# A thresholding layer between convolutions: the mixing unit takes one matrix for two images instead of two matrices for one image

## The chip, the cores and the metric

The kernel runs on one core of one Trainium2 chip, in one launch. The core has a matrix engine (TensorE, PE in the profile, with its weight loads listed apart as PEld), a vector engine (VectorE, DVE), a scalar engine (ScalarE, ACT), a general engine (GpSimd, POOL), and a queue that issues the DMA transfers (SyncE, SP). Each takes its instructions in order, and they wait for one another by semaphores. TensorE writes its products to PSUM, which has eight banks of 512 fp32 values in each of 128 partitions; everything else lies in SBUF or in DRAM. The metric is the device time of one execution in microseconds (us).

## What is computed

Four images of 64 channels of 256 x 256 values, all fp32, pass through four layers. Layers 0, 2 and 3 are long convolutions: every channel is convolved with a filter that is an outer product of a row filter and a column filter, so the kernel multiplies with two triangular Toeplitz matrices, and adds `x * bias`. Layer 1 is the one that the change touches. It goes to Haar coefficients, mixes the channels there with two 64 x 64 matrices, thresholds, and comes back:

```python
f1 = haar2d(x)
acc = jnp.zeros_like(f1[:, :conv_w.shape[1]])
for i in range(v.shape[0]):                      # two matrices
    f3 = f1 * v[i]
    f4 = jnp.einsum('bchw,oc->bohw', f3, conv_w[i])
    f5 = jnp.sign(f4) * jax.nn.relu(jnp.abs(f4) - tau[i])
    acc = acc + f5
y = haar2d(acc, inverse=True)
return y + x
```

Since `v[i]` and `tau[i]` depend on the place in the image alone and not on the channel, the kernel mixes first and multiplies with `v` afterwards; and the `+ x` is added as coefficients, before the inverse transform.

## The kernel before

Phase A is layer 0 and the forward Haar transform. It works in rounds of two channels of a pair of images (64 rounds, 32 for each pair, which is called a group). In a round the matrix engine multiplies with the row and the column filters (`toeplitz`, L307), ScalarE copies the first product to SBUF (L450), VectorE adds the residual (L470), GpSimd does the transform along the free dimension (`forward_free`, L355 and L357, sixteen operations from 128x1024 down to 128x8), TensorE does the other direction (`haar`, L319), and the result is copied out of PSUM (L483, by VectorE for a part of the rounds) and stored to a DRAM tensor `coef` (L488). Every store goes in four transfers of 64 partitions with 4 KB in a piece.

Phase B is the mixing. It needs all channels of one place, so it reads `coef` back in steps: a step is 128 partitions (two rows of the image times 64 channels) by two images by 512 values, 512 KB, 64 steps for each group. A step loads `f` (tile ft, four buffers, L546), `v` and `tau` (three buffers each, L552), and is cut into two units. In a unit of the kernel before, four matrix products (`mix`, L592) apply both matrices to one image; each occupies a 64 x 64 quarter of the array, and TensorE runs each as two instructions. Then follow `multiply` with v on VectorE, in place in PSUM (L603), the sign on ScalarE to an SBUF tile m (L609), the magnitude on ScalarE, in place in PSUM (L612), `less` on VectorE (subtraction of tau, in place in PSUM, L616), and `threshold` on VectorE, which multiplies the clipped magnitude with the sign into m (L619). The PSUM tile f4 has two buffers of two banks. It is called f in the profile, since digits are left out of names there. Of the two matrices' results one lies in the wrong half of the partitions, so for each step ScalarE copies the two halves of the second results crosswise into a tile `other` (`exchange`, L625, two copies of 64x1024), and GpSimd adds the first results and `f` (L629) and then `other` (L632) into a tile gt, which is stored to a DRAM tensor `mixed` (L635).

Phase C is the inverse transform with layers 2 and 3, again in rounds of two channels: it loads `mixed` (tile g, L699, four transfers of 256 KB), undoes the transform on GpSimd (`inverse_free`, L392) with scalings on ScalarE (L375) and on TensorE (L319, copies L728), runs four sets of Toeplitz products (c1r, c1c, c2r, c2c), with copies of ch on ScalarE (L740) and residuals on VectorE (L759), and stores the output (L766).

The order of the work is written out by hand. Every phase is a list of pieces, and `beside` issues the pieces of a main list with those of a side list spread evenly among them. As engines take their instructions in order, this order decides who stands behind whom. Phase A of the first group runs with the filter networks beside it; from round 34 on phase B of group 0 runs beside phase A of the second group; then phase C of group 0 starts, and phase B of group 1 runs beside it; the rest is phase C alone. A piece of phase B is named (u, j) here, with u the unit and j from 0 to 2, and s = u // 2 its step:

```python
(u, 0): mix(u), less(u - 1)
(u, 1): multiply(u), sign(u), threshold(u - 1); load(s + 2) in even units, add_second(s - 1) in odd ones
(u, 2): magnitude(u); exchange and add_first(s - 1) in even units, store(s - 1) in odd ones
```

The second half of the exchange stands at (u, 0) of odd units. A round of phase A is 10 pieces and one of phase C is 18. Copies out of PSUM and residuals of the phases A and C are put off to the start of the next piece (`later` and `flush`). Their PSUM tiles have four buffers of one bank (`acps`).

Of the kernel before, what the change touches and what calls it, by code (L numbers as in the profile page):

```python
# [41 lines left out]
F32 = mybir.dt.float32  # L42
# [5 lines left out]
P = 128  # L48
# [41 lines left out]
def conv_haar_kernel(  # L90
# [9 lines left out]
    def coefficients(name):  # L100
        return dram.tile([STEPS, 2, C, NB, 2, N], F32, tag=name, name=name)
# [166 lines left out]
    def copy_tau(k):  # L268
        tau_sb = thresholds[1]
        for i in range(2):  # L270

            at, half = taus.offset + (k * 2 + i) * W, 2 * W * COPIES
            by_row = [[half, 2]] if i == 0 else [[-half, 2]]
            to = bass.AP(taus.tensor, at + i * half, [[2 * half, C]] + by_row + [[1, W]])
            nc.sync.dma_start(to, tau_sb[:, 2 * i : 2 * i + 2].rearrange("p h k -> p (h k)"))
# [139 lines left out]
    def rows_of(dram_tile, c, bp):  # L415

        n = NB * W
        at = dram_tile.offset + (bp * 2 * C + c) * n
        return bass.AP(dram_tile.tensor, at, [[4 * C * n, ROW // 2], [C * n, 2], [1, n]])

    def all_rows(grp_tile, c0, images):

        parts = images.rearrange("p (s n) k -> p s (n k)", s=2)
        return [(rows_of(grp_tile, c0 + e, bp), parts[half(e), bp]) for e in range(CI) for bp in range(2)]
# [104 lines left out]
    def phase_b(grp):  # L529
# [7 lines left out]
        def step_of(ap, s):  # L537
            n = NB * W
            return bass.AP(ap.tensor, ap.offset + 2 * s * C * n, [[n, P], [1, n]])
# [14 lines left out]
        def four(name):  # L554

            tiles = [st[s][name] for s in range(2)]
            tiles.append(bp.tile([P, NB, W], F32, tag="other", name=f"spare_{name}_{grp}", bufs=2))
            return [t[:C, :, bass.ts(h, N)] for t in tiles for h in range(2)]

        def join():  # L560

            a, b, c, d, t, u = four("f")
# [9 lines left out]
        def part():  # L572

            a, b, c, d, t, u = four("g")
# [10 lines left out]
        def mix(u):  # L585
            f = st[u // 2]["f"]
            un[u]["f4"] = bps.tile([P, 2, W], F32, tag="f4", name=f"f4_{grp}_{u}")

            for i in range(2):
                for q in range(2):  # L590
                    to = (q + i) % 2
                    nc.tensor.matmul(  # L592
                        un[u]["f4"][half(to), i, :],
                        mixers[0][half(q), bass.ts(i, C)],
                        f[half(q), u % 2],
                        start=True,
                        stop=True,
                        tile_position=(q * ROW, to * ROW),
                    )

        def multiply(u):
            f4 = un[u]["f4"]
            nc.vector.tensor_tensor(f4, f4, st[u // 2]["v"], ALU.mult)  # L603
# [356 lines left out]
```

## Time and profile before

| what | us |
|---|---|
| three timed runs | 2892.87, 2900.72, 2903.77 |
| median of them | 2900.72 |
| profiled execution | 2902.61 |
| its span, first to last instruction | 2900.8 |
| PE busy, of the span | 2439.5 |
| POOL busy | 1930.3 |
| DVE busy | 1561.7 |
| ACT busy | 1523.6 |
| DMA queue q1, mean share of 16 engines | 76.3% |

Single instructions of phase B, from the groups of instructions with their shapes kept apart:

| instruction | count | mean ns |
|---|---|---|
| mix, PE, 64*64 64x512 | 2048 | 662 |
| multiply, DVE, 128x1024 | 256 | 1225 |
| sign, ACT, 128x1024 | 256 | 1029 |
| magnitude, ACT, 128x1024 | 256 | 1035 |
| less, DVE, 128x1024 | 256 | 1230 |
| threshold, DVE, 128x1024 | 256 | 1213 |
| copy of other, ACT, 64x1024 | 256 | 1046 |
| each of the two adds, POOL, 128x1024 | 128 | 2363 |

A line of a list of instructions in the profile gives the engine, the line of the kernel, the operation, what is written and what is read, and the count; in brackets stands how long the engine had been idle before and what it waited for. A line of a list of waits gives the waiting instruction, what it waited for, the total, how many times, and the longest. "issue" means that the engine waited for nothing that the profile shows. The granted clock is the share of full speed that TensorE was allowed, and the DMA share is the mean busy share of the core's 16 DMA engines.

### The profile page before, as it was taken

What the parts mean: (1) busy time and instruction counts of PE and PEld (TensorE: products, weight loads), DVE (VectorE), ACT (ScalarE), POOL (GpSimd) and SP (SyncE); (2) the same over time, 40 slices, a digit from 0 to 9 for tenths busy, and PEclk for the clock granted to TensorE, in tenths of its full rate; (3) what the DMA queues carried; (4) which work ended last, traced back from release to release, by engine and by line L of the source; (5) the groups of instructions that cost most, each with busy time, mean ns of one, the idle gap of its engine ahead of it and who ended that gap; (6) DMA issues with size and microseconds to landing.
All of it is one profiled execution on the core that took longest, in us unless ns stands there. A gap on an engine that the chain in (4) does not pass through costs nothing.

```text
span 2900.8 us, 119451 instructions
## 1 busy us (share of the span) xinstructions
PE 2439.5 (84%) x53276; PEld 1966.7 (68%) x53276; DVE 1561.7 (54%) x1765; ACT 1523.6 (53%) x2361; POOL 1930.3 (67%) x2294
## 2 busy tenths in 40 slices
PE   6999886777776777868978888888888999999999
PEld 5777775444444544546757767666677889898888
DVE  2453333777777777537656766666673333333333
ACT  1222222666776666436767776666674333433332
POOL 2787674977887877738767766766675556555551
PEclk9999998988998888979999999999999999999999
DMA  5878888899999999777989888888975555655552
GB/s 153 238 212 228 235 237 228 244 284 289 296 291 284 276 300 281 217 182 224 252 238 251 252 231 248 239 243 242 253 211 159 142 151 137 155 143 146 146 141 92
DMA packets 239673, 636.27 MB, mean 219 GB/s; under 512 B 39078, under 2 KB 121671, under 8 KB 223032
## 3 DMA queue, kind: packets, MB, share of 16 engines
q1 hardware_dynamic: 239160, 628.62, 76.3%
q8 instruction: 420, 6.88, 1.0%
q14 instruction: 93, 0.76, 0.1%
HBM read 413.12 MB, written 215.35 MB: 217 GB/s over the span
## 4 chain that ended last, share of the span: by engine, by line
PE 45%; ACT 11%; DMA 10%; issue 8%; DVE 7%; POOL 4%; SPq 2%; ACTq 0%; DVEq 0%; POOLq 0%
PE c1r L307 9%; PE c1c L307 9%; PE c2c L307 9%; PE c2r L307 8%; PE f L592 4%; PE c0ps L319 3%; DVE f L603 3%; ACT m L609 3%; ACT f L612 3%; DMA v<-in_v 3%; ACT other L625 2%; DMA ft<-coef 2%; POOL fw L355 1%; POOL f L357 1%; ACT ch L740 1%
## 5 line engine op out<-in xcount | busy, mean ns | idle before, releaser
L392 POOL TENSOR_TENSOR i<-i,g 128x16 f32<-128x16 f32 x744 | 393.1, 549 | 407.5 <-ACT g L375 397.7
L616 DVE TENSOR_TENSOR f<-f,tau 128x1024 f32<-128x1024 f32 x256 | 314.8, 1230 | 384.0 <-ACT f L612 384.0
L592 PE MATMUL f<-ft,mix 64*64 64x512 f32 x2048 | 341.1, 662 | 189.4 <-DVE m L619 102.0
L609 ACT ACTIVATE m<-f 128x1024 f32<-128x1024 f32 x256 | 263.3, 1029 | 415.8 <-DVE f L603 400.3
L307 PEld LDWEIGHTS a1ps<-tx,x 64*64 64x64 f32 x8192 | 332.7, 144 | 146.9 <-ACT f L483 65.6
L629 POOL TENSOR_TENSOR gt<-m,ft 128x1024 f32<-128x1024 f32 x128 | 302.5, 2363 | 192.9 <-DVE m L619 167.0
L307 PE MATMUL a1ps<-tx,x 64*64 64x256 f32 (+3 forms) x8192 | 363.5, 320 | 56.1 <-ACT f L483 26.0
L307 PE MATMUL c2r<-tx,cy 64*64 64x128 f32 (+3 forms) x8192 | 332.1, 305 | 50.2 <-issue 36.8
L307 PE MATMUL c1r<-tx,z 64*64 64x192 f32 (+3 forms) x8192 | 338.5, 308 | 39.2 <-issue 39.2
L307 PEld LDWEIGHTS c2r<-tx,cy 64*64 64x64 f32 x8192 | 308.9, 137 | 81.4 <-issue 48.7
L603 DVE TENSOR_TENSOR f<-f,v 128x1024 f32<-128x1024 f32 x256 | 313.6, 1225 | 91.8 <-PE f L592 64.8
L307 PEld LDWEIGHTS c1r<-tx,z 64*64 64x64 f32 x8192 | 316.3, 139 | 68.8 <-issue 51.1
L307 PEld LDWEIGHTS c1c<-ty,ch 64*64 64x64 f32 x8192 | 307.7, 135 | 64.8 <-ACT z L728 47.3
L632 POOL TENSOR_TENSOR gt<-gt,other 128x1024 f32<-128x1024 f32 x128 | 302.4, 2363 | 70.6 <-ACT other L625 68.1
L307 PE MATMUL c2c<-ty,ch 64*64 64x128 f32 (+3 forms) x8192 | 323.2, 298 | 27.5 <-issue 25.2
L307 PE MATMUL c1c<-ty,ch 64*64 64x256 f32 (+3 forms) x8192 | 335.3, 303 | 10.9 <-ACT z L728 8.8
L307 PEld LDWEIGHTS a2ps<-ty,ay 64*64 64x64 f32 x8192 | 301.5, 137 | 62.1 <-issue 35.4
L307 PEld LDWEIGHTS c2c<-ty,ch 64*64 64x64 f32 x8192 | 304.0, 134 | 50.5 <-issue 31.2
L307 PE MATMUL a2ps<-ty,ay 64*64 64x192 f32 (+3 forms) x8192 | 328.3, 304 | 10.2 <-issue 6.4
L740 ACT COPY ch<-c1r 128x512 f32<-128x512 f32 x256 | 137.6, 590 | 371.4 <-PE c1r L307 371.0
L470 DVE SCALAR_TENSOR_TENSOR x<-x,bias_sb,a2ps 128x512 f32<-128x512 f32 x256 | 179.4, 741 | 268.4 <-PE a2ps L307 252.3
L619 DVE SCALAR_TENSOR_TENSOR m<-f,m 128x1024 f32<-128x1024 f32 x256 | 310.5, 1213 | 0.1
(66 smaller groups left out, 3257.9 us busy)
## 6 DMA issues: line engine op xcount, KB each, us to landing
coef<-f SPq DMA_DIRECT2D x256, 256.0 KB, 4.9
ft<-coef SPq DMA_DIRECT2D x128, 512.0 KB, 9.1
v<-in_v SPq DMA_DIRECT2D x128, 512.0 KB, 10.0
tau<-taus SPq DMA_DIRECT2D x128, 512.0 KB, 10.6
mixed<-gt SPq DMA_DIRECT2D x128, 512.0 KB, 7.8
g<-mixed SPq DMA_DIRECT2D x256, 256.0 KB, 6.9
x<-in_x SPq DMA_DIRECT2D x63, 1024.0 KB, 9.7
out<-o SPq DMA_DIRECT2D x63, 1024.0 KB, 4.8
```

What stands on the lines that cost most here:

```text
L307: nc.tensor.matmul(ps[r][half(c), j % 2, k * ROW :], data[half(r), c, k, bass.ts(j, ROW)], t(r, c)[:, : N - k * ROW], start=k == 0, stop=k ...
L319: nc.tensor.matmul(ps[r][half(c)].rearrange("p h k -> p (h k)"), matrix[half(r)], pairs(r, c).rearrange("p h k -> p (h k)"), start=True, s ...
L392: engine.tensor_tensor(to, s, d, op)
L470: nc.vector.scalar_tensor_tensor(to, old, bias_sb[:, c : c + 1], ps, ALU.mult, ALU.add)
L592: nc.tensor.matmul(un[u]["f4"][half(to), i, :], mixers[0][half(q), bass.ts(i, C)], f[half(q), u % 2], start=True, stop=True, tile_position ...
L603: nc.vector.tensor_tensor(f4, f4, st[u // 2]["v"], ALU.mult)
L609: nc.scalar.activation(un[u]["m"], un[u]["f4"], AF.Sign)
L616: nc.vector.tensor_tensor(f4, f4, st[u // 2]["tau"], ALU.subtract)
L619: nc.vector.scalar_tensor_tensor(un[u]["m"], un[u]["f4"], 0.0, un[u]["m"], ALU.max, ALU.mult)
L629: nc.gpsimd.tensor_tensor(st[s]["g"], st[s]["m"][:, :, 0], st[s]["f"], ALU.add)
L632: nc.gpsimd.tensor_tensor(st[s]["g"], st[s]["g"], st[s]["other"], ALU.add)
L740: later(lambda y=y, ps=ps: nc.scalar.copy(y, ps))
```

## The change

A unit now applies one matrix, i = u % 2, to both images of a step. The product with v goes from PSUM to a new SBUF tile x (two buffers), with v broadcast over the images; sign and magnitude read x. The magnitude goes to a PSUM tile of its own, `a`, of two banks; f4 and `a` have one buffer each. The result tile m belongs to one unit (three buffers). What is exchanged between the halves is the second image's f, a copy of two times 64x512 in a step, and no longer the result. To make this fit, the matrix of the forward transform is permuted for one image, so that its two rows of a pair stand in exchanged halves, and v and tau are no longer laid out with reversed rows. Coefficients lie in DRAM as two steps side by side, so that a channel's piece in the store of `coef` and in the load of `mixed` is 8 KB in two transfers of a round; a step of phase B reads and writes 4-KB pieces at a distance of 8 KB. The pieces are issued in another order. The first steps' join of the low coefficients is made for each image, and starts with three steps loaded.

```diff
     def coefficients(name):
-        return dram.tile([STEPS, 2, C, NB, 2, N], F32, tag=name, name=name)
+        return dram.tile([STEPS // 2, 2, C, 2, NB, 2, N], F32, tag=name, name=name)
...
     def all_rows(grp_tile, c0, images):
-        parts = images.rearrange("p (s n) k -> p s (n k)", s=2)
-        return [(rows_of(grp_tile, c0 + e, bp), parts[half(e), bp]) for e in range(CI) for bp in range(2)]
+        n = 2 * NB * W
+        pairs = []
+        for e in range(CI):
+            at = grp_tile.offset + (c0 + e) * n
+            rows = bass.AP(grp_tile.tensor, at, [[2 * C * n, ROW // 2], [C * n, 2], [1, n]])
+            pairs.append((rows, images[half(e)].rearrange("p n k -> p (n k)")))
+        return pairs
...
         def step_of(ap, s):
             n = NB * W
-            return bass.AP(ap.tensor, ap.offset + 2 * s * C * n, [[n, P], [1, n]])
+            return bass.AP(ap.tensor, ap.offset + (s // 2 * P * 2 + s % 2) * n, [[2 * n, P], [1, n]])
...
         def mix(u):
-            f = st[u // 2]["f"]
-            un[u]["f4"] = bps.tile([P, 2, W], F32, tag="f4", name=f"f4_{grp}_{u}")
-            for i in range(2):
-                for q in range(2):
-                    to = (q + i) % 2
+            s, i = divmod(u, 2)
+            un[u]["f4"] = bps.tile([P, NB, W], F32, tag="f4", name=f"f4_{grp}_{u}", bufs=1)
+            for b in range(NB):
+                for r in range(2):
+                    q = r ^ b
                     nc.tensor.matmul(
-                        un[u]["f4"][half(to), i, :],
-                        mixers[0][half(q), bass.ts(i, C)],
-                        f[half(q), u % 2],
+                        un[u]["f4"][half(q), b, :],
+                        mixers[0][half(r), bass.ts(i, C)],
+                        st[s]["f"][half(r), b],
...
         def multiply(u):
-            f4 = un[u]["f4"]
-            nc.vector.tensor_tensor(f4, f4, st[u // 2]["v"], ALU.mult)
+            un[u]["x"] = bp.tile([P, NB, W], F32, tag="x", name=f"x_{grp}_{u}", bufs=2)
+            nc.vector.tensor_tensor(un[u]["x"], un[u]["f4"], both(u, "v"), ALU.mult)

         def sign(u):
-            if u % 2 == 0:
-                st[u // 2]["m"] = bp.tile([P, NB, 2, W], F32, tag="m", name=f"m_{grp}_{u}", bufs=2)
-            un[u]["m"] = st[u // 2]["m"][:, u % 2]
-            nc.scalar.activation(un[u]["m"], un[u]["f4"], AF.Sign)
+            un[u]["m"] = bp.tile([P, NB, W], F32, tag="m", name=f"m_{grp}_{u}", bufs=3)
+            nc.scalar.activation(un[u]["m"], un[u]["x"], AF.Sign)

         def magnitude(u):
-            nc.scalar.activation(un[u]["f4"], un[u]["f4"], AF.Abs)
+            un[u]["a"] = bps.tile([P, NB, W], F32, tag="a", name=f"a_{grp}_{u}", bufs=1)
+            nc.scalar.activation(un[u]["a"], un[u]["x"], AF.Abs)

         def less(u):
-            f4 = un[u]["f4"]
-            nc.vector.tensor_tensor(f4, f4, st[u // 2]["tau"], ALU.subtract)
+            nc.vector.tensor_tensor(un[u]["a"], un[u]["a"], both(u, "tau"), ALU.subtract)
...
-        def exchange(s, q):
-            if q == 0:
-                st[s]["other"] = bp.tile([P, NB, W], F32, tag="other", name=f"other_{grp}_{s}", bufs=2)
-            nc.scalar.copy(st[s]["other"][half(q)], st[s]["m"][half(1 - q), :, 1])
-
-        def add_first(s):
-            st[s]["g"] = bp.tile([P, NB, W], F32, tag="gt", name=f"gt_{grp}_{s}", bufs=3)
-            nc.gpsimd.tensor_tensor(st[s]["g"], st[s]["m"][:, :, 0], st[s]["f"], ALU.add)
-
-        def add_second(s):
-            nc.gpsimd.tensor_tensor(st[s]["g"], st[s]["g"], st[s]["other"], ALU.add)
+        def exchange(s):
+            st[s]["other"] = bp.tile([P, W], F32, tag="other", name=f"other_{grp}_{s}", bufs=2)
+            for q in range(2):
+                nc.scalar.copy(st[s]["other"][half(q)], st[s]["f"][half(1 - q), 1])
+
+        def add(u):
+            s, i = divmod(u, 2)
+            m = un[u]["m"]
+            if i:
+                nc.gpsimd.tensor_tensor(st[s]["g"], st[s]["g"], m, ALU.add)
+            else:
+                g = st[s]["g"] = bp.tile([P, NB, W], F32, tag="gt", name=f"gt_{grp}_{s}", bufs=3)
+                nc.gpsimd.tensor_tensor(g[:, 0], m[:, 0], st[s]["f"][:, 0], ALU.add)
+                nc.gpsimd.tensor_tensor(g[:, 1], m[:, 1], st[s]["other"], ALU.add)
+            un[u].clear()
...
+        def piece(u, j):
+            s, i = divmod(u, 2)
             if j == 0:
                 if u < units:
                     multiply(u)
                     sign(u)
+            elif j == 1:
+                if 0 < u <= units:
+                    less(u - 1)
+                if i == 0 and s < STEPS:
+                    exchange(s)
+                if 1 < u <= units + 1:
+                    add(u - 2)
+            else:
                 if 0 < u <= units:
                     threshold(u - 1)
+                if u < units:
+                    magnitude(u)
+                if u + 1 < units:
+                    mix(u + 1)
+                if i == 0 and s > 0:
+                    load(s + 2)
+                if i and s > 0:
                     if s == 2:
                         part()
                         store(0)
                     if s > 1:
                         store(s - 1)
...
-            for s in range(4):
+            for s in range(3):
                 load(s)

-        pieces += [start] + [lambda: None] * 3 + [join]
-        for u in range(units + 3):
+        pieces += [start] + [lambda: None] * 3 + [lambda: [join(b) for b in range(NB)], lambda: mix(0)]
+        for u in range(units + 2):
```

## The prediction

> **What bounds the kernel now.** I read the page first: no engine is full over the span (PE 84%, POOL 67%, DVE 54%), so a mean says nothing, and I cut the span into stages. In the windows view a row gives busy microseconds of PE, PEld, DVE, ACT and POOL, the granted clock, the DMA share and GB/s.
>
> ```profile
> 0.00:470.00 470.00, 411.80 (x9381) 339.41 (x9385) 173.63 (x255) 116.99 (x211) 316.91 (x534) 0.97 0.77 219
> 470.00:1190.00 720.00, 510.36 (x8355) 336.40 (x8351) 519.48 (x496) 486.57 (x599) 558.85 (x567) 0.89 0.93 279
> 1190.00:1300.00 110.00, 74.34 (x1326) 50.44 (x1320) 36.78 (x66) 35.16 (x67) 56.24 (x92) 0.80 0.68 180
> 1300.00:2180.00 880.00, 748.82 (x15780) 610.73 (x15776) 585.50 (x600) 616.54 (x907) 620.00 (x580) 0.95 0.86 240
> 2180.00:2900.00 720.00, 694.17 (x18462) 629.70 (x18456) 246.31 (x350) 268.29 (x581) 378.27 (x522) 1.00 0.53 141
> ```
>
> The change lies in row two (layer 0 beside wavelet group 0, "A+B") and row four (layers 2 and 3 beside group 1, "C+B"). Rows one and five are PE's. In A+B PE is busy only 71%, and DMA is at 0.93. The list of waits of PE, 550 to 1150 us, says what PE waits for (us, times, longest):
>
> ```profile
> PE f L592 <- DVE m L619: 93.1, 62, 3.7
> PE f L592 <- DMA ft<-coef: 35.2, 17, 3.5
> PE a1ps L307 <- ACT f L483: 22.2, 11, 4.5
> ```
>
> The timeline there shows the ring behind the first line (start, duration; "f" is the PSUM tile f4):
>
> ```profile
> 801.50 1.21 DVE L619 SCALAR_TENSOR_TENSOR m<-f,m 128x1024 f32<-128x1024 f32 x1
> 802.05 1.05 ACT L609 ACTIVATE m<-f 128x1024 f32<-128x1024 f32 x1
> 802.96 1.05 ACT L612 ACTIVATE f<-f 128x1024 f32<-128x1024 f32 x1
> 803.90 1.10 ACT L483 COPY f<-a3ps 128x512 f32<-128x512 f32 x2
> 804.05 1.23 DVE L616 TENSOR_TENSOR f<-f,tau 128x1024 f32<-128x1024 f32 x1 [1.34 <-ACT f L612]
> 805.19 1.22 DVE L603 TENSOR_TENSOR f<-f,v 128x1024 f32<-128x1024 f32 x1
> 806.32 1.21 DVE L619 SCALAR_TENSOR_TENSOR m<-f,m 128x1024 f32<-128x1024 f32 x1
> ...
> 807.59 1.09 PE L592 MATMUL f<-ft,mix 64*64 64x512 f32 x8 [1.02 <-DVE m L619]
> ```
>
> After the threshold DVE idles 1.34 us for the magnitude of the same unit; then less, multiply, threshold; only now has PE a free f4. The ring multiply, sign, magnitude, less is 1.22 + 1.03 + 1.03 + 1.23 = 4.5 us and some 0.3 for handing over. 128 units in 700 us are 5.47 us each, so ring and DMA (0.93 of 5.47 = 5.1 us a unit) both stand near the pace.
>
> In C+B PE's own list (1300 to 2150 us) is another:
>
> ```profile
> PE c1r L307 <- issue: 38.3, 16, 3.8
> PE c2c L307 <- issue: 25.2, 18, 3.3
> PE c2r L307 <- issue: 21.5, 13, 3.0
> PE c0ps L319 <- ACT ch L740: 12.2, 10, 2.1
> PE c2r L307 <- ACT ch L740: 9.5, 4, 8.7
> PE c1c L307 <- ACT z L728: 8.8, 14, 1.3
> ```
>
> No wait for DVE's m. PE 85% busy and these waits fill the stage. The "issue" gaps recur about every 7 us, inside runs of one kind of matmul; I read them as PE out of instructions while DMA is loaded, which the change doesn't touch.
>
> **What the Trainium skill says.** "VectorE: DVE Perf Modes" (Why PSUM operands drop a tier) holds an fp32 operation with a PSUM operand at one element a cycle; its side-by-side table gives tensor_tensor two only in 16 bits. So the product to SBUF is no faster: the trace has 1225 ns in place and 1213 for the threshold, PSUM to SBUF. "PSUM — Partial Sum Buffer" (PSUM bank collisions) wants two engines kept apart by bank and quadrant, not by address: so while the magnitude lies in f4, PE can't refill it (the 93 us above); with the product in SBUF and the magnitude in banks of its own, multiply alone frees f4. "ScalarE: Activation LUTs" (Step-by-step) calls PSUM ScalarE's nearer side; here 1029 ns from PSUM against 1059 for a 128x1024 scaling in SBUF (g). "DMA: Bandwidth & Descriptors" (Why small descriptors are slow) puts a fixed cost on each packet. The trace has no such row, so I solve 16 x share x time = a x packets + b x MB for pairs of stretches: 0 to 470 with 490 to 1190 us (46205 packets, 101.42 MB, 0.764; 60474, 194.74, 0.918) gives 26 ns a packet and 45 us a MB of one engine; 2300 to 2700 with 600 to 1100 us (28090, 57.37, 0.553; 44155, 142.81, 0.944) gives 49 ns and 38 us. That is an estimate, used as a pair of bounds.
>
> **Part by part.**
>
> Mixing, product, magnitude. PE keeps eight instructions a unit in the same four quadrants. f4 has one buffer, freed by multiply; mix(u+1) comes two pieces later. Order on DVE is now multiply(u), less(u-1), threshold(u-1). Magnitude(u) waits for threshold(u-1), as `a` is single, but runs 1.03 us under multiply(u+1), 1.22 us, before less(u) wants it. So the 1.3 us stall goes and DVE's need falls to 3 x 1.22 = 3.67, with residuals (105 x 0.74 / 128 = 0.6) 4.3 us a unit. The magnitude's wait holds back ScalarE's copies queued behind it (ay, f, ch, z), and PE waits for their banks.
>
> Exchange. 256 copies of 1046 ns become 256 of 64x512: 590 (ch row) to 646 (g row, SBUF to SBUF); I take 620. ScalarE loses 256 x 0.43 = 109 us; sign from SBUF adds 0 to 0.03 x 256 = 8. At 68 to 70% it bounds nothing, so the gain is only in queued copies.
>
> Adds. Per step 2 x 2.363 = 4.73 us become 2 x 1.28 (row i 128x512) + 2.36 = 4.93: POOL +0.2 x 128 = 25 us, in idle time; without that cover 12 us a stage. POOL then needs (558.85 + 12) / 128 = 4.46 us a unit.
>
> Buffers and loads. Result m has three tiles of a unit, was two of a step: sign(u) must see add(u-3), issued two pieces before, where it had five. The first matmul on f[s+2] comes nine pieces after its load, was eleven: at 1.82 us a piece 16.4 us, was 20.1. Loads land in 7.2 to 9.7 us (medians 600 to 1100), so it should hold; 17 were late already. SP keeps its order f, v, tau; each load is one piece later behind layer 0's DMAs, and the store sits where it was, one piece behind its add.
>
> 8-KB pieces. 16,384 packets each of coef stores and g loads halve. In A+B 104 stores save 104 x 32 = 3,328 packets x 26 to 49 ns / 16 = 5 to 10 us of DMA time; C+B the like. The other side is f and mixed, now 4-KB runs at 8-KB steps: no row has that. I take no cost; ends: -5 us, or 10% dearer on 0.5 of the 1.52 MB a unit (194.74 / 128), 3% of DMA time, +20 a stage.
>
> Join. Seven operations (4.6 us) become fourteen of 64x256, some 0.42 each (padded row): +1.3 us per group, +3, with PE waiting.
>
> Sum. In A+B compute would allow about 4.5 us a unit, so DMA takes over. From 560 to 1190 us, after the start, its share is 0.95: 630 x 0.95 = 598, less 8 is 590; at 0.975 (best 100 us: 0.98) 605: -25. In C+B, PE's ScalarE waits are 30 us in 850; lighter copies and earlier products give back half: -15. Join +3. Nothing in rows one, three and five, where PE or the hand-over is late and packets are not. Total -37: the profiled execution took 2902.6 (span 2900.8), so 2866; the median shown is 1.9 lower, so 2864.
>
> **Rivals.**
>
> More: PE regains the waits for ScalarE that its weight loads show in C+B (35 + 34 + 13 = 82 us) and, less idle, is granted 0.98 instead of 0.95 (3% of 749 us = 23): two thirds of 105 is 70, 55 beyond mine; A+B at 0.99 (590 / 0.99 = 596) another 9: 2800. For: weight loads feel waits that busy matmuls hide. Against: "issue" stays, DMA at 0.86 rises.
> No change: A+B is DMA's already and the shorter lead eats what is left: 2899. For: 0.93 to 0.98, waits for ft and v of 35 and 25 us. Against: DVE's 93 us of PE's waits.
> Slower: sign waits for POOL. forward_free issues 1.9, 1.9, 1.04 and 1.04 us within two pieces of layer 0 (5.1 us), with an add of 2.4 between; inverse_free ends with two of 2.38. A lag over two pieces (3.6 us) less the add's 2.4 stops ScalarE and all copies behind it, so PE. It decides when POOL's lag passes some 5 us, slack of the copies' banks included; at 1.5 us a round, 26 + 30 rounds: +84, less my 40 of gain: 2946. For: POOL 86% busy at the new pace. Against: adds no longer wait for `other` (24 and 44 us).
>
> **Numbers.** Mine 0.48, its own range 2830 to 2890; more 0.11; no change 0.13; slower 0.28. A measurement tells about 0.5%, 14.5 us, from no change: faster, below 2886, takes mine (but 0.03) and more: 0.56; same 0.15; slower 0.29. The range is 2805 to 2945: it leaves out half of "more" and half of "slower", 0.055 + 0.14 = 0.195.
>
> **What would show it.** Right: DVE's idle before less falls from 140 us in A+B below 40, "PE f <- DVE m" goes, DMA waits (ft, v) grow, share 0.96 or above. The copies of `other` near 620 ns, adds 1.28. Wrong: ScalarE waiting for POOL's gt before sign, PE waiting for `f` or `ay` copies longer than 22 us, DMA busy longer in all, or C+B shorter than 850 us.

## The result and the profile after

| | before | after |
|---|---|---|
| median, us | 2899.92 (4 runs) | 2970.32 (4 runs, 2961.24 to 2976.68) |
| ratio, with 95% interval | | 1.0243 [1.021, 1.0277] |
| profiled execution, us | 2902.61 | 2976.68 |
| its span, us | 2900.8 | 2974.9 |

The change costs 70 us, outside the forecast range of 2805 to 2945. Executions in which a slower state of the chip showed are left out of every median and ratio below (one of the four of e2). The windows of the kernel after, cut as the prediction cut those of before (busy us of PE, PEld, DVE, ACT and POOL, granted clock, DMA share, GB/s):

```profile
0.00:470.00 470.00, 407.52 (x9377) 334.07 (x9380) 172.20 (x254) 117.04 (x211) 316.90 (x534) 0.98 0.79 220
470.00:1190.00 720.00, 516.56 (x8140) 341.18 (x8136) 521.29 (x495) 437.50 (x588) 555.38 (x614) 0.84 0.94 274
1190.00:1300.00 110.00, 70.51 (x1274) 51.96 (x1266) 37.95 (x65) 34.08 (x61) 65.38 (x103) 0.81 0.67 185
1300.00:2180.00 880.00, 734.15 (x15609) 600.01 (x15609) 588.15 (x601) 567.53 (x905) 615.19 (x634) 0.95 0.87 238
2180.00:2900.00 720.00, 660.56 (x16953) 587.57 (x16957) 237.18 (x330) 259.29 (x560) 377.90 (x522) 0.97 0.53 137
```

The last row is the surprise. There only phase C runs, no unit of the mixing is left, and DMA stands at 0.53 as before; yet PE runs 16953 matmul instructions in it where it ran 18462, with more idle time and a lower clock. Between the issues of the output stores, which mark the rounds of phase C, the 74 us of span lie here (us):

| stretch | before | after | more |
|---|---|---|---|
| start to first output store | 1332 | 1345 | 13 |
| 25 rounds beside the mixing (C+B) | 25 x 31.65 | 25 x 31.80 | 4 |
| the next 3, in which the mixing ends | 79.7 | 93.8 | 14 |
| the next 32, phase C alone | 32 x 20.24 | 32 x 21.61 | 44 |

What PE waits for in A+B (550 to 1150 us; us, times, longest):

```profile
PE f L587 <- DMA ft<-coef: 121.8, 38, 6.7
PE a1ps L304 <- ACT f L479: 22.4, 11, 3.1
...
PE f L587 <- DVE m L616: 3.0, 1, 3.0
```

The wait for DVE's m went from 93.1 us to 3.0, as intended. The wait for f itself grew from 35.2 us to 121.8: one wait took the other's place. In phase C alone, first after (2270 to 2900 us, 30 us more than the other stretch), then before (2250 to 2850 us):

```profile
PE c2r L304 <- issue: 22.9, 11, 2.7
PE c1c L304 <- issue: 11.6, 12, 2.0
PE c0ps L316 <- issue: 8.2, 4, 2.8
```

```profile
PE c2r L307 <- issue: 11.6, 10, 2.2
PE c0ps L319 <- issue: 2.2, 2, 1.2
```

13.8 us of "issue" became 42.7 (40.0 in 600 us, 2270 to 2870): PE stood with nothing the profile shows to wait for. The chain of waits of the kernel after has them on the path, one in each of these two rounds (start, duration, what):

```profile
2523.99 1.46 PE c1c L304 x29
2525.45 0.81 issue
2526.26 3.22 PE c1c L304 x68
...
2544.85 0.92 PE c1c L304 x14
2545.76 1.08 issue
2546.84 3.76 PE c1c L304 x86
```

Such a gap cuts a run of equal matmuls at a place that no operand explains. I numbered PE's instructions from the trace (a weight load and its matmul count two, every other instruction of PE's queue one). Of the 42 gaps above 0.75 us between weight loads (from start to start) from 2270 to 2870 us, 24 stand at number 193 or 194 of a cycle of 256, and these hold 50.2 of the 64.6 us; before (2250 to 2850 us), it is 12 of 40 with 20.2 of 41.8 us. So the gaps elsewhere are no more than they were, and those at one place in 256 grew by 30 us. The DMA queue that carries instructions (q8) moves packets of 16384 bytes; before (packets, MB, share of the DMA engines' time):

```profile
q8 instruction: 420, 6.88, 1.0%
```

PE has 107506 instructions there, 419.9 times 256: q8 brings PE its instructions, 256 in a packet, 64 bytes each. I read the gaps as PE's next packet of instructions arriving late, and call them **late fetches** below: gaps above 0.5 us at these places, counted from 650 to 50 us before the end, 13 with 20.9 us before and 27 with 49.9 us after.

The times of q8's packets bear this out. All 27 late fetches after end 1.27 to 1.69 us after the end of a packet, and it is always the packet whose turn it is when both are counted from the start. No packet in this stretch starts before PE has come to number 193 of its cycle (194 after), one whole cycle before PE needs it, so I take that place as the earliest time at which it can have been asked for. From there to the start of the packet it is 1.30 us on average before and 1.80 after, and above 3 us for 17 of 124 packets before and for 32 of 115 after; the packet itself then takes 1.13 and 1.14 us. During the waits above 3 us the 16 engines were 0.93 busy with the other transfers (q1), before and after; where the packet started within 0.5 us, they were 0.24 and 0.23 busy in the 2 us from that place on. So the packets of instructions start late, and they do so while the engines are full of data.

The prices of the new operations, ScalarE's and then VectorE's (count | busy us, mean ns | idle before, releasers):

```profile
L606 ACT ACTIVATE m<-x 128x1024 f32<-128x1024 f32 x256 | 271.2, 1059 | 343.7 <-DVE x L602 256.1 <-POOL gt L628 39.2 <-POOL gt L632 24.0
L610 ACT ACTIVATE a<-x 128x1024 f32<-128x1024 f32 x256 | 264.2, 1032 | 211.5 <-DVE m L616 210.4
L622 ACT COPY other<-ft 64x512 f32<-64x512 f32 x256 | 158.0, 617 | 3.8
```

```profile
L613 DVE TENSOR_TENSOR a<-a,tau 128x1024 f32<-128x1024 f32 x256 | 313.9, 1226 | 41.2 <-ACT a L610 41.1
```

The issues of the loads of mixed, after and before (transfers, KB each, median us to landing):

```profile
g<-mixed SPq DMA_DIRECT2D x128, 512.0 KB, 8.8
```

```profile
g<-mixed SPq DMA_DIRECT2D x256, 256.0 KB, 6.9
```

### The profile page after: what moved, and what is told of

Read it like the earlier page. It is cut to its first block, busy times and chain, and to the rows that moved or that the text cites. A ratio compares the mean times of both kernels' runs of the same rounds, so it can differ in the third digit from the quotient of the medians.

```text
span 2974.9 us, 119229 instructions
## 1 busy us (share of the span) xinstructions
PE 2459.2 (83%) x53276; PEld 1979.5 (67%) x53276; DVE 1583.0 (53%) x1779; ACT 1434.8 (48%) x2361; POOL 1946.2 (65%) x2422
## 4 chain that ended last, share of the span: by engine, by line
PE 48%; DMA 16%; issue 8%; DVE 6%; POOL 5%; ACT 4%; SPq 1%; DVEq 0%; ACTq 0%; POOLq 0%
PE c1c L304 10%; PE c1r L304 9%; PE c2c L304 9%; PE c2r L304 8%; PE f L587 4%; DMA ft<-coef 4%; DMA v<-in_v 4%; PE c0ps L316 3%; DMA mixed<-gt 2%; DVE x L602 2%; DMA x<-in_x 2%; PE a2ps L304 1%; POOL fw L352 1%; DMA tau<-taus 1%; PE a1ps L304 1%
## 5 line engine op out<-in xcount | busy, mean ns | idle before, releaser
L602 DVE TENSOR_TENSOR x<-f,v 128x1024 f32<-128x1024 f32 x256 | 312.6, 1221 | 344.1 <-PE f L587 275.9
L587 PE MATMUL f<-ft,mix 64*64 64x512 f32 x2048 | 357.1, 682 | 166.8 <-DMA ft<-coef 130.4
L606 ACT ACTIVATE m<-x 128x1024 f32<-128x1024 f32 x256 | 271.2, 1059 | 343.7 <-DVE x L602 256.1
L304 PE MATMUL a1ps<-tx,x 64*64 64x192 f32 (+3 forms) x8192 | 367.9, 317 | 46.5 <-ACT f L479 23.4
L304 PE MATMUL c2r<-tx,cy 64*64 64x256 f32 (+3 forms) x8192 | 329.9, 303 | 50.4 <-issue 39.9
L304 PE MATMUL a2ps<-ty,ay 64*64 64x128 f32 (+3 forms) x8192 | 343.2, 309 | 29.1 <-issue 21.9
L610 ACT ACTIVATE a<-x 128x1024 f32<-128x1024 f32 x256 | 264.2, 1032 | 211.5 <-DVE m L616 210.4
L304 PE MATMUL c1c<-ty,ch 64*64 64x256 f32 (+3 forms) x8192 | 341.9, 302 | 26.2 <-issue 19.9
L613 DVE TENSOR_TENSOR a<-a,tau 128x1024 f32<-128x1024 f32 x256 | 313.9, 1226 | 41.2 <-ACT a L610 41.1
L616 DVE SCALAR_TENSOR_TENSOR m<-a,m 128x1024 f32<-128x1024 f32 x256 | 313.2, 1223 | 21.7
L628 POOL TENSOR_TENSOR gt<-gt,m 128x1024 f32<-128x1024 f32 x128 | 302.9, 2366 | 19.9 <-DVE m L616 16.1
## 6 DMA issues: line engine op xcount, KB each, us to landing
ft<-coef SPq DMA_DIRECT2D x128, 512.0 KB, 11.1
```

The source lines that it names most:

```text
L304: nc.tensor.matmul(ps[r][half(c), j % 2, k * ROW :], data[half(r), c, k, bass.ts(j, ROW)], t(r, c)[:, : N - k * ROW], start=k == 0, stop=k ...
L587: nc.tensor.matmul(un[u]["f4"][half(q), b, :], mixers[0][half(r), bass.ts(i, C)], st[s]["f"][half(r), b], start=True, stop=True, tile_posi ...
L602: nc.vector.tensor_tensor(un[u]["x"], un[u]["f4"], both(u, "v"), ALU.mult)
L606: nc.scalar.activation(un[u]["m"], un[u]["x"], AF.Sign)
L610: nc.scalar.activation(un[u]["a"], un[u]["x"], AF.Abs)
L613: nc.vector.tensor_tensor(un[u]["a"], un[u]["a"], both(u, "tau"), ALU.subtract)
```

## The experiments

Each ratio is against the kernel before on the same chip in the same batch, whose median drifted between 2889.7 and 2899.9; so runs of different batches are best compared by their ratios. "A+B" is the time of the first output store, "late" the us of late fetches in phase C alone. These and the rounds come from one profiled execution of each run, which lies up to 15 us from the run's median.

| run | built on | median | ratio [95%] | A+B | C+B round | C alone round | late |
|---|---|---|---|---|---|---|---|
| before | | 2899.92 | 1 | 1332 | 31.65 | 20.24 | 20.9 |
| after | | 2970.32 | 1.0243 [1.021, 1.0277] | 1345 | 31.80 | 21.61 | 49.9 |
| e1_pieces_4k | after | 2927.28 | 1.0114 [1.006, 1.0167] | 1335 | 31.98 | 20.20 | 22.7 |
| e2_before_8k | before | 2963.47 | 1.0256 [1.0199, 1.0312] | 1348 | 31.78 | 21.44 | 47.0 |
| e3_loads_4k | after | 2924.92 | 1.0102 [1.0061, 1.0143] | 1334 | 31.71 | 20.34 | 24.3 |
| e4_f_early | after | 2943.22 | 1.0158 [1.0117, 1.0199] | 1320 | 31.78 | 21.51 | 52.0 |
| e5_two_by_512k_4k | after | 2952.00 | 1.0209 [1.0176, 1.0243] | 1333 | 31.75 | 21.36 | 47.3 |
| e7_four_by_256k_8k | after | 2934.93 | 1.0138 [1.0098, 1.0178] | 1350 | 32.09 | 20.49 | 30.7 |
| e8_loads_4k_f_early | e3 + e4 | 2892.75 | 1.0003 [0.998, 1.0026] | 1318 | 31.66 | 20.44 | 26.5 |
| e9_e8_b_ends_early | e8 | 2888.65 | 0.9989 [0.9967, 1.0011] | 1320 | 31.96 | 20.26 | 23.1 |
| e10_two_spaced | after | 2970.16 | 1.0278 [1.025, 1.0306] | 1333 | 32.04 | 21.42 | 48.4 |
| e11_before_f_early | before | 2876.05 | 0.9952 [0.9924, 0.998] | 1320 | 31.55 | 20.11 | 17.6 |
| e12_v_tau_spread | e9 | 2902.31 | 1.005 [1.0028, 1.0072] | 1342 | 32.04 | 20.24 | 24.5 |
| e13_v_tau_g_spread | e12 | 2909.89 | 1.0073 [1.0053, 1.0094] | 1322 | 32.37 | 20.10 | 22.7 |
| e14_two_apart | after | 2905.61 | 1.0056 [1.0036, 1.0075] | 1331 | 30.90 | 20.52 | 32.5 |
| e15_eight_by_128k | e11 | 2864.56 | 0.9896 [0.9864, 0.9928] | 1323 | 31.21 | 19.71 | 7.0 |
| e16_f_v_tau_halves | e11 | 2863.67 | 0.9909 [0.9877, 0.9941] | 1309 | 31.28 | 20.17 | 16.8 |
| e17_eighths_and_halves | e15 + e16 | 2865.83 | 0.9916 [0.9889, 0.9944] | 1303 | 31.81 | 19.72 | 7.2 |
| e18_changed_eighths | e8 | 2867.43 | 0.9927 [0.9899, 0.9955] | 1315 | 31.08 | 19.94 | 12.6 |
| e19_two_apart_f_early | e4 + e14 | 2884.43 | 0.9982 [0.9963, 1.0002] | 1302 | 30.83 | 20.75 | 32.0 |

Where an expectation names a theory by a letter: P is the length of a packet (8 KB hold up a fetch longer than 4 KB), S the size of one transfer, B the burst, the bytes handed to the queue within a short time.

### Which part costs

The pieces of 8 KB were undone on the kernel after, for stores and loads:

```diff
+            for bp in range(2):
+                at = grp_tile.offset + (c0 + e) * n + bp * n // 2
+                rows = bass.AP(grp_tile.tensor, at, [[2 * C * n, ROW // 2], [C * n, 2], [1, n // 2]])
+                pairs.append((rows, parts[half(e), bp]))
```

> The changed kernel, but coefficient stores and loads of mixed go in four transfers of 4-KB pieces again (the DRAM layout of the change stays). Theory F (8-KB packets of these transfers hold up TensorE's instruction fetches, so issue gaps grow): the stage of layers 2 and 3 alone goes from 21.6 us a round back to 20.3, 34 rounds, so about -45 there and some -10 in the other stages: near 2915 us. Theory O (the unit's new order is what costs): nothing moves, 2970 us.

In the kernel before they were made alone: the new `coefficients`, `all_rows` and `step_of`, and nothing of the unit.

> The kernel before with the new DRAM layout and 8-KB pieces alone. Theory F: the stage of layers 2 and 3 alone goes from 20.3 to about 21.6 us a round, total about 2950 us. Theory O: 2900 us, within 0.5%.

In the third only the loads of `mixed` went back to 4 KB in four transfers of 256 KB (`half_rows`, the four lines above under another name, used in phase C's `load` alone).

> The changed kernel with only the loads of mixed (phase C) in 4-KB pieces; the coefficient stores keep 8 KB. Theory F: nearly all of the gain of the four-transfer version, as the lost time lies in the stage of layers 2 and 3 alone: about 2925 us. Theory O: 2970 us.

e2 alone costs 64 us by its median and 74 by its ratio, about as much as the whole change; e1 gives back 43 us and e3 45, so no part of the stores of `coef` shows. The waits of PE in phase C alone of e2 (2250 to 2900 us):

```profile
PE c2r L307 <- issue: 23.4, 11, 5.0
PE c0ps L319 <- issue: 11.9, 4, 3.9
PE c1c L307 <- issue: 4.4, 8, 1.8
```

The old unit with the new loads has the gaps of the kernel after (39.7 us in 650). So two loads of 512 KB in the place of four of 256 KB cost about 44 us. The two transfers differ in three things, in size, in burst and in packet; the next runs take these apart.

### The load of f

```diff
+        def load_f(s):
+            if s < STEPS:
+                d = st[s]
+                d["f"] = bp.tile([P, NB, W], F32, tag="ft", name=f"ft_{grp}_{s}", bufs=4)
+                nc.sync.dma_start(d["f"].rearrange("p b w -> p (b w)"), step_of(coef[grp], s))
...
                 if i == 0 and s > 0:
                     load(s + 2)
+                    load_f(s + 3)
```

> The changed kernel with f loaded a step earlier (its four buffers allow it); v and tau as they are. Theory L (the shorter lead of f costs in the stage with phase A): TensorE's waits for ft there fall from 122 us below 40 and the kernel gains 15 to 25 us, 2950 us. If that stage is bound by the DMA engines (share 0.95), the waits move to v or to a copy and the time stays at 2970 us.

27 us, and nearly all in A+B: the first output store comes at 1320. PE's waits in A+B of e4 (550 to 1150 us):

```profile
PE f L591 <- DVE x L606: 48.0, 34, 4.5
PE a1ps L304 <- ACT f L479: 32.5, 19, 3.3
PE a2ps L304 <- ACT ay L446: 32.1, 28, 2.5
PE a3ps L316 <- DVE x L466: 26.6, 15, 4.4
```

The waits for ft are gone. The other waits, for VectorE and ScalarE, grew from 38.5 us (160.3 in all with ft) to 139.2, so little idle time is saved in the window; but it holds 5% more work (7269 matmuls in place of 6916), at a clock of 0.89 for 0.84 and a DMA share of 0.97 for 0.96. Both repairs together:

> The changed kernel with loads of mixed in four transfers of 4-KB pieces and f loaded a step earlier. The two repairs lie in different stages (layers 2 and 3; phase A of the second group), so they should add: 2970 - 45 - 27 = 2898 us, the time of the kernel before within 0.5%.

They add: 2892.75, a ratio of 1.0003, equal to the kernel before. Then the same early f in the kernel before, whose buffers allow it too:

> The kernel before with f loaded a step earlier, nothing else. If its stage with phase A was held by the ring through the single f4 and the magnitude, only the 35 us of waits for ft are to be had and most come back as waits for m: 0 to -10 us, 2885 us where the kernel before has 2891. If the DMA lead was all that mattered, it gains like the changed kernel, -25 us.

The old unit gains 0.5% with it, about half of what the new one gained, and its first output store is at 1320 as well. So e8 and e11, which differ in the unit and the layout in DRAM but not in the transfers of `mixed` nor in f, stand at 1.0003 [0.998, 1.0026] and 0.9952 [0.9924, 0.998]: like for like the change is slower. Over all runs with f early and group 0 otherwise alike, that store comes at 1315 on average with the new unit (1320, 1318, 1320, 1315, 1302: e4, e8, e9, e18, e19) and at 1314 with the old (1320, 1323, 1309, 1303: e11, e15, e16, e17). The new unit with its layout is worth nothing in A+B. The two weren't parted: no run has the new unit with the old layout, so the 8-KB pieces of `coef` could hide a gain of the unit (e2, the layout with the old unit, has that store at 1348). The scatter also says that the 13 us between 1332 and 1345 are one draw: e3, e5, e7, e10 and e14, which have the same first part as the kernel after, lie from 1331 to 1350.

### The end of the mixing

```diff
-    beside(main, phase_b(1), len(c_first) + 2 * BLOCKS + 6, 0)
+    beside(main, phase_b(1), len(c_first) + 2 * BLOCKS + 6, 8)
```

> As the version with both repairs, but the mixing of group 1 ends eight pieces of phase C sooner. Theory E (the last store of mixed stands now at the very end of the list, before it stood some 4 pieces ahead, so that phase C of group 1 starts late): another 8 to 12 us, about 2888 us. Otherwise 2898 us.

The three rounds in which the mixing ends took 90.8 us in e8 and take 77.2, below the kernel before (79.7). The 25 rounds ahead take longer, 31.96 for 31.66; by the medians 4 us are left of 13.6, and the two intervals overlap.

### Packet, size or burst

Two transfers of 512 KB whose rows are walked with the two halves in reverse order, so that each packet is 4 KB again (82304 packets of 4 KB in the trace, as in e3, where the kernel after has 65920); and four transfers of 32 partitions, with packets of 8 KB:

```diff
+            at = grp_tile.offset + (c0 + e) * 2 * n + n
+            rows = bass.AP(grp_tile.tensor, at, [[2 * C * n, ROW], [-n, 2], [1, n]])
+            pairs.append((rows, parts[half(e), ::-1]))
```

```diff
+            for k in range(2):
+                at = grp_tile.offset + (c0 + e) * n + k * ROW // 4 * 2 * C * n
+                rows = bass.AP(grp_tile.tensor, at, [[2 * C * n, ROW // 4], [C * n, 2], [1, n]])
+                start = e * ROW + k * ROW // 2
+                pairs.append((rows, images[start : start + ROW // 2].rearrange("p n k -> p (n k)")))
```

> The changed kernel; the loads of mixed stay two transfers of 512 KB a round, but their 8-KB rows are walked as two 4-KB pieces, second piece first, so that the packets are 4 KB. Theory P (the length of the packets holds up the instruction fetches): like the version with four transfers of 4-KB pieces, 2925 us, 20.4 us a round in the stage of layers 2 and 3 alone. Theory T (two large transfers put more bytes in the queues at once than four small ones): no gain, 2970 us, 21.6 us a round.

> The changed kernel; the loads of mixed go in four transfers of 256 KB a round, each of 32 partitions with 8-KB packets. Theory P: still slow, 2970 us and 21.6 us a round in the stage of layers 2 and 3 alone. Theory T: 2925 us, 20.4 us a round.

(T in these two stands for S and B together.) In phase C alone, 512 KB with short packets stay at 21.36, and 256 KB with long ones fall to 20.49. P falls, up to a few tenths of a us a round. Then the two transfers of 512 KB were drawn apart, first by issuing the second three pieces later.

> The changed kernel; the two 512-KB loads of mixed with their 8-KB packets stay, but the second is issued three pieces of phase C (some 4 us) after the first. Theory B (a burst: 1 MB issued in 2 us queues faster than the engines drain it, and the instruction fetch waits behind the backlog): the stage of layers 2 and 3 alone comes back to 20.3 to 20.5 us a round, 2930 us. Theory S (the size of a single transfer is what matters): stays at 21.4 us a round, 2970 us.

Nothing moved, and the timeline of SyncE says why. The kernel after, then e10 (start, duration of the issues together, count):

```profile
2515.10 2.36 SPq L694 DMA_DIRECT2D g<-mixed  x2
```

```profile
2501.63 2.84 SPq L695 DMA_DIRECT2D g<-mixed  x2
```

SyncE runs ahead of the other engines, and three pieces without an instruction that holds it aren't time: both are still issued within 2.84 us. So e10 says nothing of B. In e14 the first half goes in between the filter loads four pieces earlier, and these wait for their tiles:

```diff
                 filters(t + 1, 1)
+                if t + 3 != alone:
+                    load(t + 3, slice(0, 1))
                 filters(t, 2)
...
-                load(t + 3)
+                load(t + 3, slice(1, 2))
```

> The changed kernel with its two 512-KB loads of mixed, 8-KB packets, but the first half now stands among the filter loads four pieces earlier, where the queue itself has to wait; so the halves go out some 10 us apart (the version with the second half three pieces later had them back to back, since SyncE runs ahead). Theory B (1 MB at once): 20.3 to 20.5 us a round in the stage of layers 2 and 3 alone, 2930 us. Theory S (the size of one transfer, 32 KB for each DMA engine): stays at 21.4 us a round, 2970 us.

```profile
2502.69 0.53 SPq L695 DMA_DIRECT2D g<-mixed  x1
...
2517.09 0.46 SPq L695 DMA_DIRECT2D g<-mixed  x1
...
2522.28 0.53 SPq L695 DMA_DIRECT2D g<-mixed  x1
```

In this timeline of e14 the transfers follow one another after 14 and 5 us by turns. With the same 512 KB and the same packets of 8 KB, C alone falls from 21.61 to 20.52, the late fetches from 49.9 to 32.5 us, and the whole by 54 us as the ratios have it (1.0243 and 1.0056). The first half also has a longer lead here, and its place among the filter loads is another; neither was tried alone. With f early:

> The changed kernel with f a step early and its two loads of 512 KB about 14 us apart. Burst in time decides (theory B): the gains add, 2943 less 65 gives 2878, at or below the 2893 of four transfers of 256 KB back to back. Size of a transfer decides (theory S): a 512-KB transfer is as harmful alone, so above 2893, about 2910.

2884.43 (0.9982), where S expected 2910 and four transfers of 256 KB back to back gave 2892.75 (1.0003). In phase C alone two transfers of 512 KB drawn apart take back 0.8 to 1.1 us a round of the 1.1 to 1.3 that four of 256 KB do, so the burst decides most of it; the late fetches stay somewhat above those of e3 and e8 (32 us beside 24 to 27), which leaves S a part. About 22 us of the gain in the whole lie in C+B (31.80 to 30.9 and 30.83 a round), though the late fetches of its first 780 us hardly change there (131.7 us after; 129.0 in e14, 124.3 in e19); what it is there stays open.

### Smaller transfers

Since a transfer of 512 KB is itself a burst, the loads of `mixed` were cut to eight of 128 KB, on the old unit and on the new one:

```diff
+                for k in range(2):
+                    at = grp_tile.offset + (bp * 2 * C + c0 + e) * n + k * ROW // 4 * 4 * C * n
+                    rows = bass.AP(grp_tile.tensor, at, [[4 * C * n, ROW // 4], [C * n, 2], [1, n]])
+                    start = e * ROW + k * ROW // 2
+                    pairs.append((rows, parts[start : start + ROW // 2, bp]))
```

> The kernel before with f early, and loads of mixed in eight transfers of 128 KB (8 KB for each DMA engine) instead of four of 256 KB. Theory S: late fetches in the stage of layers 2 and 3 alone fall from 18 us in 600 to 10 or less, 20.1 us a round to 19.9, some -8 us: 2868 us. Theory B: the loads are spread over 5 us of issue instead of 3.3, about the same -8 us. If neither: 2876 us, or more where SyncE's extra issues make the filters late.

> The changed kernel with f a step early and mixed loaded in eight transfers of 128 KB instead of two of 512 KB; layout in DRAM and the new unit stay. Four transfers of 256 KB gave 2893. If the size of a transfer counts on below 256 KB in this unit as it did in the old one (12 us), 2880 and C alone 19.7 to 19.9; if the new unit has a cost of its own, it stays some 15 us above the old unit with the same loads (2864.6); if the units are worth the same, it equals it.

e15 is faster than both kernels. Against e11 it is 0.9896 for 0.9952, some 16 us, with intervals that just meet; its late fetches in phase C alone fall from 17.6 to 7.0 us, in the first 780 us of C+B from 134 to 48. Whether size or spacing does it, this run can't tell. The issue now spreads the megabyte over 6.89 us:

```profile
2512.10 6.89 SPq L720 DMA_DIRECT2D g<-mixed  x8
```

The DMA's busy tenths in 40 slices of 2250 to 2800 us, of the kernel after and of e15, show the same bytes laid out:

```profile
DMA  7537165374573553726736617537367355373673
```

```profile
DMA  5546536535545654644663654554455375355454
```

e18 has the new unit with the same loads: 0.9927 [0.9899, 0.9955] beside e15's 0.9896 [0.9864, 0.9928]. The change has no gain left to show. Next, the mixing's own loads of group 1, f, v and tau, each in two of 256 KB, and then both edits:

```diff
+                for r in range(2) if grp else ():
+                    n = NB * W
+                    src = bass.AP(coef[grp].tensor, coef[grp].offset + (2 * s + r) * C * n, [[n, C], [1, n]])
+                    nc.sync.dma_start(d["f"][half(r)].rearrange("p b w -> p (b w)"), src)
...
+                    for i in range(2):
+                        flat = bass.AP(src.tensor, at + i * W, [[2 * W, 2 * COPIES], [0, C // COPIES], [1, W]])
+                        nc.sync.dma_start(t[:, i], flat)
```

> The kernel before with f early, and for group 1 the loads of f, v and tau in two transfers of 256 KB each instead of one of 512 KB (16 KB for each DMA engine; v and tau with 2-KB packets). Theory S: late fetches in the stage of layers 2 and 3 beside the mixing fall from 134 us in 780 to about 90, 31.55 us a round to 30.5, and the kernel gains some 25 us: 2850 us. Theory B: the three loads still go out together, no gain, or a loss of 5 to 10 us by the smaller packets: 2876 to 2886 us.

> The kernel before with f a step early, mixed loaded in eight transfers of 128 KB, and group 1's f, v and tau each in two of 256 KB (the two edits of the two runs before together). If each cures late fetches of its own transfers, the gains of 11 and 12 us over 2876 add: about 2852, C alone 19.7 us a round, late fetches in C+B below 48 us. If they share one gain (in C+B both thin the same fetches), about 2862, and C+B stays at 31.2 us a round.

e16 lies 12 us below e11, with intervals that overlap, and 12 us of its profiled execution's gain are in A+B, where the edit changes nothing. The late fetches of C+B fell from 134 us to 96, and a round only from 31.55 to 31.28. The gains don't add: 2865.83. In e17 the late fetches of C+B are down to 15.5 us, yet a round there takes 31.81. PE's waits from 1300 to 2130 us of e17 show what came next:

```profile
PE c2r L307 <- ACT ch L771: 75.8, 25, 6.3
PE c0ps L319 <- ACT ch L771: 12.8, 15, 1.6
PE c1c L307 <- ACT z L759: 9.9, 14, 1.8
PE c2r L307 <- issue: 5.3, 6, 2.1
```

ScalarE's copy of ch, 9.5 us of waits before c2r in the kernel before, is what PE waits for in C+B once the instructions come in time. This is where the old unit's heavier exchange on ScalarE could begin to tell; a unit with lighter copies in e17's loads wasn't tried.

Two runs put v, tau and, in the second, the four transfers of `mixed` into pieces of their own:

> The version with loads in 4 KB, f early and the mixing ending early; v and tau are issued one and two pieces after f instead of with it. Theory B: the 1.5-MB burst of a step is broken up, late fetches in the stage with layers 2 and 3 (some 130 us of issue gaps in 780 us) fall by a third or more, and the kernel gains 20 to 40 us: 2860 us. Theory S, or a stage held by the total of DMA: no gain, 2889 us.

> As the version with v and tau spread, and the four loads of mixed of a round go one a piece over four pieces. Theory B: another 5 to 15 us, from the stages with phase C, 2850 us. Theory S: no change from that version.

Both were slower than e9. Their timelines have e10's fault: in e13 the four loads of `mixed` in phase C alone are still issued within 3.2 us (near 2508 us), and in the first 780 us of C+B f and the v and tau nearest to it start within 3.5 us of one another in e12 and 3.4 in e13 (medians), where e9 had 4.5. They moved instructions and drew nothing apart, so they say nothing against B; why they are slower than e9 stays open.

## Why the prediction was wrong

Against the forecast sum of -37 us the span grew by 74. By stages, phase C alone missed by 44 us, A+B by 38 (+13 for -25), C+B by 19 (+4 for -15) and the end of the mixing by 14.

**"Nothing in rows one, three and five, where PE or the hand-over is late and packets are not."** This is the step that failed most, 44 us of the 74 of span. Row five was costed by DMA's share, 0.53, and a share is a mean over 720 us: within a round two transfers of 512 KB come at once, and PE's next instructions come by DMA too. The prediction had seen the issue gaps and had read them as PE out of instructions under a loaded DMA, "which the change doesn't touch". The change touched just that load. The windows from 2250 to 2800 us, before and after:

```profile
2250.00:2800.00 550.00, 536.71 (x14289) 486.07 (x14291) 189.14 (x270) 210.22 (x461) 307.21 (x432) 1.00 0.56 146
```

```profile
2250.00:2800.00 550.00, 513.92 (x13325) 459.82 (x13321) 175.93 (x251) 195.78 (x430) 284.64 (x402) 0.98 0.53 136
```

PE was busy 536.71 us of 550 before and 513.92 after; by round, 19.75 and 20.19 busy, 0.49 and 1.42 idle. So 0.93 us a round are gaps, and 0.44 a lower clock (0.98 for 1.00, 2% of 19.75 is 0.40). That late fetches make up the gaps is read from their place in 256 and from the packets' ends; that they wait behind data, from the packets' late starts beside a data share of 0.93, and from the runs that changed only how the data is handed over. It agrees with what the Trainium skill says in "DMA: Bandwidth & Descriptors" (Queues, rings and completion order), that an engine with several queues drains a packet of one before it turns to the next. The trace doesn't record when a packet was asked for, only that none started before the place named above; the packet itself isn't slower once begun (1.13 us before, 1.14 after).

**The 8-KB pieces, "-5 to -10 us" of DMA time a stage.** Not there: loads of 4 KB in e3 and of 8 KB in the kernel after took about 308 and 632 ns a packet in phase C alone, twice the time for twice the bytes. (The output's 8-KB packets, in both kernels, lie near 310 ns, so that the loads' are read as the slower group.) The estimate of 26 to 49 ns a packet came from stretches with other mixes of packets, and the same page's fixed cost for each packet (Why small descriptors are slow) is not visible between 4 and 8 KB here. f's dearer 4-KB steps at 8-KB distance, the prediction's upper bound, weren't measured alone.

**Buffers and loads, "so it should hold".** It did not; issuing f a step earlier gave 27 us back (e4). The prediction counted the lead in pieces, 20.1 us before and 16.4 after, against landings of 7.2 to 9.7 us, medians again. The traces have no such lead: from 550 to 1150 us the median time from ft's issue to the first matmul on it, waits included, was 8.7 us before and 11.5 after (14.3 in e4), so SyncE issued the loads later than the order of the pieces suggests. ft landed in a median of 11.1 us after against 9.1, and 38 loads were late by up to 6.7 us.

**Mixing, product, magnitude, "A+B -25".** The mechanism came: VectorE's wait for the magnitude before less fell from 118.5 us to 25.8 (550 to 1150 us; 384.0 to 41.2 in the whole), and "PE f <- DVE m" from 93 to 3. No time came of it: the old unit with f early, and with the old layout, reaches the same 1314 us. DMA's share from 550 to 1150 us is 0.95 to 0.97 in both kernels and in the runs with f early, and it moves 293 to 299 GB/s in those, whichever the unit. This fits the prediction's own view that DMA takes over; that DMA holds both units to the same time is argued from these figures.

**C+B "-15".** Not there (31.80 for 31.65). PE's waits there were first of all late fetches, 119 us before and 132 after in the first 780 us. Yet they alone weren't the limit either: e17 is nearly rid of them (15.5 us), PE waits for ScalarE's ch in their place, and a round is no shorter. What holds C+B to some 31 us stays open.

**Not in the sum:** the mixing's last units stand at the very end of the list, worth 14 us in the profile of after; e9 took that stretch back, with little of it in the whole.

**Right:** the copies of `other` 617 ns (forecast 620), the adds 1275 to 1277 and 2366, sign from SBUF 1059, DMA waits for f and v grown. **The rival "slower"** named the right sign for the wrong cause: ScalarE waits for POOL before sign 63 us in all (39.2 + 24.0), against a price of 84 us on the path, and e8, with the causes of these waits in place, is at 1.0003. They may have a part in the 0.5% between e8 and e11 (0.3% between e18 and e15, whose intervals overlap). No run took them out alone.

## What to carry to other kernels

Before transfers are made larger, look for an "issue" gap of PE at a fixed distance in instructions, and for the packets of the instruction queue just before it ends. Here what counted then was mostly how many bytes were handed over at once, not the mean share or the length of packets. Spread such loads in time, or cut them; and look in the issuing queue's timeline whether an edit moved time at all, since a queue that runs ahead undoes a new order. When a ring of waits is taken out, ask whether the old form with only its loads earlier would come as far.

## What the runs showed of the hardware

Smaller transfers were faster here. With a megabyte loaded for each round of phase C alone, as two transfers of 512 KB back to back, four of 256 KB and eight of 128 KB, a round took 21.4 to 21.6, 20.1 to 20.5 and 19.7 to 19.9 us. The Trainium skill's rule in "DMA: Bandwidth & Descriptors" (Bandwidth, Measured) to batch to 1 MiB or more is one for bandwidth; at a share of 0.53 bandwidth was not what was short, and the measurement decides for the smaller ones here.

PE's instructions came in packets of 16 KB, some 420 in the whole span and 1.0% of the DMA engines' time, and the waits for them took 20.9 us of 600 in a stretch of the kernel before where PE is 98% busy.

A median of 2865 us, 1% under the kernel before, was reached by three versions of the kernel before (e15, e16, e17): f loaded a step earlier, and smaller transfers. With the change and the same two remedies (e18) it is 2867.
